# Unpaced gathers, an opening in two SBUF regions, and first layer-1 strips ahead, in a sparse two-layer graph kernel

## The chip, the cores and the metric

The kernel runs on one core of one Trainium2 chip. The metric is device time in microseconds of one execution. Before the change it was 2570.24 us, the median of 14 runs (2565.58 to 2576.75).

## The reference

A graph of 3327 nodes with 128 features goes through two layers, each with a layer norm and a ReLU ahead of it and a residual around it. Layer 0 is an attention layer (GATv2) of four heads over a weighted adjacency; layer 1 is a graph convolution over the same adjacency.

```python
h = maximum(layernorm(x), 0)
# layer 0, for each of 4 heads
E = leaky_relu((h @ w1)[:, None, :] + (h @ w2)[None, :, :], 0.01)
s = exp(tanh((E @ a) / 8) * 8) * adj
out = leaky_relu((s / s.sum(-1, keepdims=True)) @ h @ Wlin.T, 0.01)
x = x + concatenate(outs, -1) @ w
# layer 1
h = maximum(layernorm(x), 0)
A_t = adj + eye(n);  D_inv = rsqrt(A_t.sum(1))
x = x + relu((D_inv[:, None] * A_t * D_inv[None, :]) @ (h @ W.T + b))
```

About 2% of the adjacency is not zero, so a node has some 64 neighbours. Scores are needed for those pairs only.

## The kernel before, in words

Nodes are padded to 3328 = 26 blocks of 128. Layer 0 goes block by block, and each block is done in two halves (`hb`) of 64 rows. For a half, the neighbours' rows are gathered from a table in device memory by indirect DMA, which GpSimd (POOL) issues. A table row holds 720 floats (2880 B): 64 edge weights, 128 features of the node, a few scalars, and the four projections `h @ w2`. There are two such tables, one for each half: the features are the same, but the 64 edge weights in front are rewritten for each block (`weights`, L554: a DMA on SP's queue that reads the transposed adjacency `AT_d` and writes the first 256 B of every row).

The neighbour lists of a half fill 32 gathers of 128 rows, in 4 windows (`w`) of 8 gathers, and 3 more gathers (`ge`) hold what overflows: 35 a half, 70 a block, 1820 in all. A window's 8 gathers land in one buffer `g` of 23040 bytes a partition; there are 4 such buffers in the pool `pg`, and one of `ge`. A window is two groups (`m`) of TensorE work, the overflow one, so a half has 9 groups and a block 18. A group is:

- `stage_z` (L562): TensorE transposes the gathered projections into PSUM (`z`, L573), and VectorE takes the maximum with `x1n` (`r`, L585, 128x1024 at a time, two in a group).
- `stage_r` (L591): TensorE multiplies `r` with the score vector (`s`, L597).
- `finish` (L601), a generator in steps: copy, transpose, tanh and exp, weights `wt`, and the aggregation `ag` (L645, L663), after which the buffer is free (`allow`).
- `close` (L669), another generator, once a half or block is aggregated: output projection, residual, layer norm of layer 1, its product with `W`, and at last (L736) the block's rows of layer 1's right side into `x_sb`. The block is then `closed`.

Beside the groups of one block runs `prep` of the next (72 steps, half a block ahead): load of its adjacency rows (`load`, L334, 1.7 MB into the single buffer `adjb`), transposes of it to `AT_d`, the sparse index lists by repeated maxima of eight, and small products.

The order is written out by hand (`manual_schedule`): every engine runs its instructions in the order of the program. The function `slot` (L806) is called six times a group; it takes a step of every open `finish` and `close`, advances `prep`, and calls `fetch` and `trickle`. `fetch` (L770) puts the gathers of a window into `queue` when a buffer is free. `trickle` (L795) issues from the queue by a credit of `RATE = 0.7` gathers a slot, and `issue` (L788) makes each gather wait for the latest maximum `r` in program order (`state["pace"]`).

```python
def trickle():
    state["credit"] = min(2.0, state["credit"] + RATE) if queue else 0.0
    while queue and (state["credit"] >= 1 or queue[0][0] is None):
        state["credit"] -= queue[0][0] is not None
        issue()
```

In the opening (pool `pre`) the node features are normalised, and for 7 groups of four blocks `features`, `turn`, `products` (L971) and `store` (L967) make the table rows in `img` (5 buffers) and write each to both tables (1312 KB each), on SP's queue. `AT_d` of block 0 and the first two `weights` come before. When `pre` closes, `pg` is opened in its place.

Layer 1 (`layer1`, L859) multiplies strips: for each strip `s` of four blocks (512 columns of `AT_d`), one matmul (L870) for each column block `j` that is not in the partial sum `part1` already (`finished`: the blocks closed before the strip's rows were prepared). That is 26, 24, 20, 16, 12, 8 and 4, or 110 column blocks of 256 KB. They are loaded in pieces of up to 11 into `g` buffers (`strip`, L820) once the last gathers are issued, and multiplied while the last block is being closed and after it. The last column of strip 0 waits until every block is closed.

Of the kernel before, what the change touches and what calls it, by code (L numbers as in the profile page):

```python
# [227 lines left out]
def _sparse_layers(tc, nc, x, adj, w1, w2, a, wlin, w, gw, gb, gb_sb, gwT, x_sb, dinv, flag, ident, out):  # L228
# [24 lines left out]
    with ExitStack() as l0:  # L253
# [4 lines left out]
        xn_d = dram.tile([NP, D], F32, name="xn_d")  # L258
        part1_d = dram.tile([D, NP], F32, name="part1_d")
        NS = -(-NB // 4)  # L260
        AT_d = dram.tile([NS * NP, 4 * P], F32, name="AT_d")
# [76 lines left out]
        def prep(b, k):  # L338
# [6 lines left out]
            def tables_step(j0):  # L345
                n = min(4, NB - j0)
                pt = ps_tr.tile([P, 4, P], F32, name="tr")
                for q in range(n):
                    nc.tensor.transpose(pt[:, q, :], adjb[:, (j0 + q) * P:(j0 + q + 1) * P], ident)  # L349
                at = pat.tile([P, 4, P], F32, name="at") if b else blks[0].pool.tile([P, 4, P], F32, name="at0", bufs=4)  # L350
                nc.scalar.copy(at[:, :n, :], pt[:, :n, :])  # L351
                at0 = (b // 4) * NP
                eng = nc.scalar if b else nc.sync
                eng.dma_start(AT_d[at0 + j0 * P:at0 + (j0 + n) * P, b % 4 * P:b % 4 * P + P].rearrange("(b p) c -> p b c", p=P),
                                  at[:, :n, :])
                js = range(min(n, finished(b) - j0))
                if len(js):
                    known.append(known_step(j0, js, at))
# [56 lines left out]
            k.turned = True  # L415
            hTb = pb.tile([P, P], F32, name="hTb")
            nc.sync.dma_start(hTb, hT_d[:, b * P:(b + 1) * P])
            nc.scalar.activation(adjb, adjb, AF.Copy, accum_out=deg)
# [115 lines left out]
            nc.scalar.copy(pex, pm[:, :16 * H].rearrange("p (t h) -> p t h", h=H))  # L534
            k.x1b, k.x1n, k.pex, k.hTb = x1b, x1n, pex, hTb
            yield

        def gather(b, hb, w):

            k = blks[b]  # L540
            tab = tables[hb]
            if w == NW:
                g, n, at = pe_.tile([P, OVT, ROW], F32, name="ge"), OVT, k.idxo[:, hb]
            else:
                g, n, at = pg.tile([P, WT, ROW], F32, name="g"), WT, k.idx[:, w, WT * hb:WT * hb + WT]

            def one(t):
                return nc.gpsimd.indirect_dma_start(out=g[:, t, :], out_offset=None, in_=tab[:, :],  # L548
                                                    in_offset=bass.IndirectOffsetOnAxis(ap=at[:, t:t + 1], axis=0))

            queue.extend((k, hb, w, partial(one, t)) for t in range(n))
            k.g[hb, w] = g
# [9 lines left out]
        def stage_z(k, hb, m, slot):  # L562
# [4 lines left out]
            for hp in range(2):  # L567
# [15 lines left out]
                else:  # L583
                    r0 = HALF * hb + 32 * (m % 2)
                    made = nc.vector.tensor_tensor(r.rearrange("p h (i s) -> p h i s", s=16), z.rearrange("p h (i s) -> p h i s", s=16),  # L585
                                            k.x1n[:, 2 * hp:2 * hp + 2, r0:r0 + 32, None].to_broadcast([P, 2, 32, 16]), OP.max)
                    state["pace"] = made.ins.name
                out.append(r)
# [165 lines left out]
        state = {"slot": 0, "fetched": 0, "g": 4, "ge": 1}  # L754
        state["pace"], state["credit"] = None, 0.0
        RATE = 0.7
        SYNC = mybir.DependencyInfo(mybir.DependencyClass.Sync, mybir.DependencyReason.DATA)
        ends, tails = [], []
# [29 lines left out]
        def issue():  # L788

            what, _, _, make = queue.popleft()  # L790
            made = make()
            if what is not None and state["pace"] is not None:
                tc.add_manual_dep(made.ins, state["pace"], SYNC, reason="pace")

        def trickle():  # L795
            state["credit"] = min(2.0, state["credit"] + RATE) if queue else 0.0
            while queue and (state["credit"] >= 1 or queue[0][0] is None):
                state["credit"] -= queue[0][0] is not None
                issue()
# [6 lines left out]
        def slot():  # L806
# [5 lines left out]
            fetch()  # L812
            trickle()


        PIECE = 11
        pieces = [(s, j0, min(PIECE, NB - j0)) for s in range(NS) for j0 in range(finished(4 * s), NB, PIECE)]
        strips = {}

        def strip(s, j0, n):  # L820
            g = pg.tile([P, WT, ROW], F32, name="g")
            v = g.rearrange("p t c -> p (t c)")[:, :n * 4 * P].rearrange("p (j i) -> p j i", j=n)
            w = min(4, NB - 4 * s) * P
            for k, lo in enumerate(range(0, n, 4)):
                hi = min(n, lo + 4)
                eng = nc.scalar if k % 2 else nc.sync
                eng.dma_start(v[:, lo:hi, :w], AT_d[s * NP + (j0 + lo) * P:s * NP + (j0 + hi) * P, :w].rearrange("(j p) i -> p j i", p=P))
            strips[s, j0] = v

        def strip_in(s):  # L830
# [6 lines left out]
            if finished(4 * s):  # L837
                nc.sync.dma_start(r1[:, 0], part1_d[:, rows].rearrange("p (b i) -> p b i", b=n))
            return n, rows, r0, r1

        def strip_out(s, po, n, rows, r0, r1):

            ot, t, xo = r0[:, 1], r1[:, 1], r0[:, 0]
            po = po[:, :n * P].rearrange("p (b i) -> p b i", b=n)
            if finished(4 * s):
                nc.vector.tensor_add(ot, po, r1[:, 0])
            else:
                nc.scalar.copy(ot, po)
# [10 lines left out]
        def layer1():  # L859
            ending = []  # L860
            for s in range(NS):
                w = min(4, NB - 4 * s) * P
                po = ps_z.tile([P, 2, BANK], F32, name="z")[:, 0]
                j1 = finished(4 * s)
                ins = strip_in(s)
# [11 lines left out]
            for e in ending:  # L877
                for _ in e:
                    pass

        groups = [(b, hb, m) for b in range(NB) for hb in range(2) for m in range(NG)]
        fetches = [(b, hb, w) for b in range(NB) for hb in range(2) for w in range(NW + 1)] + [(NB, 0, i) for i in range(len(pieces))]

        with tc.tile_pool(name="pre", bufs=1) as pre:
            blks[0].pool = pre
            w2_sb = pre.tile([P, H, D], F32, name="w2_sb")
            nc.scalar.dma_start(w2_sb, w2.rearrange("h k d -> k h d"))
            a_bc = pre.tile([P, H, D], F32, name="a_bc")
            spans = [(lo, min(hi, NB)) for lo, hi in ((0, 4), (4, 12), (12, NB)) if lo < NB]
            x_v = x.rearrange("(b p) d -> p b d", p=P)  # L890
            for lo, hi in spans:
                nc.sync.dma_start(x_sb[:, lo:hi, :], x_v[:, lo:hi, :])
# [15 lines left out]
            wa = pre.tile([P, 3 * H], F32, name="wa")  # L908
            zero = pre.tile([1, ROW // 6], F32, name="zero")
            nc.vector.memset(zero, 0.0)  # L910
            nc.sync.dma_start(tables[0][NP:NP + 1, :].rearrange("r (k u) -> r k u", k=6), zero[:, None, :].to_broadcast([1, 6, ROW // 6]))
            nc.sync.dma_start(tables[1][NP:NP + 1, :].rearrange("r (k u) -> r k u", k=6), zero[:, None, :].to_broadcast([1, 6, ROW // 6]))

            def norm(b0, n):
# [10 lines left out]
                for _ in inv_root(rstd, var):  # L925
                    pass
                cen = pre.tile([P, n, D], F32, name=f"cen{b0}")
                for k in range(n):
# [6 lines left out]
            def weights_of_scores():  # L935


                prod = pre.tile([P, H, D], F32, name="prod")
                nc.vector.tensor_mul(prod, w2_sb, a_bc)
# [9 lines left out]
            def features(i):  # L949

                b0, n = 4 * i, min(4, NB - 4 * i)
                img = pre.tile([P, 4, ROW - FEAT], F32, name="img", bufs=5)
                nc.gpsimd.memset(img[:, :n, P + H:PROJ - FEAT], 1.0)
# [4 lines left out]
            def turn(i):  # L958
                b0, n = 4 * i, min(4, NB - 4 * i)
                pt = ps_s.tile([P, BANK], F32, name="s")  # L960
                for k in range(n):
                    nc.tensor.transpose(pt[:, k * P:(k + 1) * P], imgs[i][:, k, :P], ident)
                hTs[i] = pre.tile([P, BANK], F32, name="hT", bufs=2)
                nc.scalar.copy(hTs[i][:, :n * P], pt[:, :n * P])
# [6 lines left out]
            def products(i):  # L971
# [18 lines left out]
                store(i, 0)  # L990
                if i:
                    store(i - 1, 1)

            wlin_sb = pre.tile([P, H, D], F32, name="wlin_sb")
            nc.sync.dma_start(wlin_sb, wlin.rearrange("h o d -> o h d"))
# [23 lines left out]
            with tc.manual_schedule():  # L1019
# [18 lines left out]
                weights(0, 1)  # L1038
                turn(0)
                weights_of_scores()  # L1040
                if len(spans):
# [8 lines left out]
                for i in range(1, K):  # L1050
# [3 lines left out]
                    advance(2 + NCODE * i / (K - 1))  # L1054
                    ahead(i + 4)
                store(K - 1, 1)
                advance(NLIST)
                turn_parameters()
                if NB > 1:
                    load(1)  # L1060
                advance(NPREP)

        pg = l0.enter_context(tc.tile_pool(name="pg", bufs=4))

        with tc.manual_schedule():
# [5 lines left out]
            for i in range(-1, n + 1):  # L1071
                if i + 1 < n:
                    slot()
                if 0 <= i < n:
                    b, hb, m = groups[i]
                    rs[i] = stage_z(blks[b], hb, m, slot)
                if 0 <= i - 1 < n:
# [6 lines left out]
            todo = "one"  # L1084
            while ends or tails:
                slot()
# [143 lines left out]
```

## Time and profile before

| | |
|---|---|
| median of 14 runs | 2570.24 us (2565.58 to 2576.75) |
| the profiled execution | 2572.91 us; its span, first to last instruction, 2571.2 us |
| mean granted TensorE clock | 0.978 |
| busy share | PE 89%, DVE 79%, POOL 70%, ACT 27% |
| DMA | 867.74 MB, mean 337 GB/s |
| DMA queues, share of 16 engines | gathers (q0) 71.8%, SP (q1) 18.4%, ACT (q10) 7.1% |
| first gather starts, last gather ends | 85.6 us, 2435.5 us |

PE, PEld, DVE, ACT, POOL and SP are TensorE's matmuls, its weight loads, VectorE, ScalarE, GpSimd and the sync engine. A line of the costliest groups reads: line, engine, operation, out<-in, count | busy us, mean ns of one | idle time of the engine just before them, and what ended most of it. "issue" means that the engine waited for nothing that the profile shows. A line of the timeline has start and duration in us, and in brackets the idle time before it and its releaser. A line of the waits has total us, times, and the longest. A line of the stages has the stretch and its length, then busy us and number of instructions of each engine, the granted clock, the DMA share and GB/s. A line of the chain has start, length, and the work on it.

### The profile page before, as it was taken

How to read it: one execution, taken by the hardware profiler on the slowest of the kernel's cores; microseconds unless marked ns; L12 is line 12 of the kernel's file. 1: busy time of each engine (PE TensorE's matmuls, PEld its weight loads, DVE VectorE, ACT ScalarE, POOL GpSimd, SP SyncE). 2: the span in 40 equal slices, each digit the busy share in tenths (PEclk: the TensorE clock that was granted, in tenths of full speed). 3: DMA queues.
4: the chain of work that ended last, by engine and by line, in shares of the span. 5: the costliest groups of instructions: out<-in, count | busy, mean ns of one | idle time of the engine just before them, and what ended most of it. 6: DMA issues, size and time to landing. Idle time of an engine off the chain costs nothing.

```text
span 2571.2 us, 52428 instructions
## 1 busy us (share of the span) xinstructions
PE 2291.4 (89%) x19410; PEld 1594.4 (62%) x19410; DVE 2027.1 (79%) x6256; ACT 700.6 (27%) x1648; POOL 1796.0 (70%) x1865
## 2 busy tenths in 40 slices
PE   6689998888988998999999999899999989998898
PEld 3456666665666666666666666667666666766543
DVE  5788988788887878879888888878888788896512
ACT  3222233223223322322322232232223223222110
POOL 3577777777777777777777777777777777777600
PEclk8699999999999999999999999999999999999999
DMA  9999999999999999999999999999999999999976
GB/s 316 353 350 330 351 361 331 339 365 347 324 352 350 332 343 365 334 333 355 356 331 341 375 337 337 359 353 329 342 371 334 329 354 351 337 316 325 308 270 216
DMA packets 459768, 867.74 MB, mean 337 GB/s; under 512 B 208877, under 2 KB 317937, under 8 KB 456177
## 3 DMA queue, kind: packets, MB, share of 16 engines
q0 software_dynamic: 145600, 671.04, 71.8%
q1 hardware_dynamic: 217360, 136.76, 18.4%
q10 hardware_dynamic: 96544, 56.50, 7.1%
q8 instruction: 156, 2.56, 0.4%
q14 instruction: 108, 0.88, 0.1%
HBM read 795.84 MB, written 112.63 MB: 353 GB/s over the span
## 4 chain that ended last, share of the span: by engine, by line
DVE 28%; DMA 27%; PE 25%; POOL 10%; issue 9%; ACT 0%; DVEq 0%; SPq 0%; ACTq 0%; POOLq 0%
DMA g<-table,idx 20%; DVE r L585 12%; POOL g L548 8%; PE z L573 7%; DMA ge<-table,idxo 4%; PE s L597 4%; DVE cand L399 4%; PE z L870 4%; PE z L576 3%; DVE codes L395 2%; PE tr L614 2%; DMA AT_d<-at 1%; PE ag L645 1%; POOL ge L548 1%; PE tr L496 1%
## 5 line engine op out<-in xcount | busy, mean ns | idle before, releaser
L548 POOL DMA_INDIRECT g<-table,idx x1664 | 1618.5, 973 | 558.1 <-issue 359.3
L573 PE MATMUL z<-ident,g 128*128 128x128 f32 x6656 | 929.7, 279 | 184.5 <-DVE r L585 121.6
L585 DVE TENSOR_TENSOR r<-z,x1n 128x1024 f32<-128x1024 f32 x832 | 1009.3, 1215 | 32.7 <-PE z L573 30.5
L573 PEld LDWEIGHTS z<-ident,g 128*128 128x128 f32 x6656 | 746.2, 143 | 395.2 <-DVE r L585 248.3
L597 PE MATMUL s<-r,sel 128*32 128x512 f32 (+1 forms) x3744 | 489.2, 595 | 0.7 <-ACT ssb L605 0.7
L617 DVE TENSOR_TENSOR sc<-tr,g 128x32 f32<-128x32 f32 x208 | 38.6, 186 | 328.4 <-PE tr L614 328.4
L605 ACT COPY ssb<-s 128x512 f32<-128x512 f32 x260 | 146.9, 565 | 513.9 <-PE s L597 509.2
L399 DVE MAX8 cand<-codes 128x8 f32<-128x52 uint16 x1664 | 215.4, 205 | 0.0
L548 POOL DMA_INDIRECT ge<-table,idxo x156 | 154.9, 993 | 47.5 <-issue 35.9
L625 ACT ACTIVATE th<-sc 128x32 f32<-128x32 f32 x260 | 58.3, 224 | 446.8 <-DVE sc L620 441.1
L576 PE MATMUL z<-oi,x1b 128*128 128x384 f32 x416 | 175.0, 503 | 0.0
L645 PEld LDWEIGHTS ag<-g,wt 128*32 128x32 f32 x3328 | 98.8, 110 | 113.4 <-issue 98.9
L351 ACT COPY at<-tr 128x512 f32<-128x512 f32 (+1 forms) x182 | 101.0, 555 | 221.1 <-PE tr L349 187.6
L614 PE MATMUL tr<-ident,ssb 128*128 128x128 f32 x988 | 154.6, 277 | 4.4 <-ACT ssb L605 3.0
L573 PEld LDWEIGHTS z<-ident,ge 128*128 128x128 f32 x624 | 82.0, 147 | 108.2 <-DMA ge<-table,idxo 34.8
L582 ACT ACTIVATE r<-z 128x768 f32<-128x768 f32 x104 | 84.4, 811 | 217.7 <-PE z L576 217.7
L597 PEld LDWEIGHTS s<-r,sel 128*32 128x32 f32 x3744 | 73.8, 108 | 110.0 <-issue 85.9
L573 PE MATMUL z<-ident,ge 128*128 128x128 f32 x624 | 114.4, 284 | 30.3 <-DMA ge<-table,idxo 27.9
L645 PE MATMUL ag<-g,wt 128*32 128x133 f32 x3328 | 133.5, 278 | 0.0
L614 PEld LDWEIGHTS tr<-ident,ssb 128*128 128x128 f32 x988 | 115.6, 142 | 14.2 <-ACT ssb L605 12.5
L349 PE MATMUL tr<-ident,adjb 128*128 128x128 f32 x676 | 106.6, 280 | 16.4 <-DMA adjb<-in_adj_dram 10.2
L395 DVE SCALAR_TENSOR_TENSOR codes<-adjb,code 128x832 uint16<-128x832 f32 x104 | 102.3, 1021 | 1.5 <-DMA adjb<-in_adj_dram 1.5
(177 smaller groups left out, 2343.8 us busy)
## 6 DMA issues: line engine op xcount, KB each, us to landing
adjb<-in_adj_dram SPq DMA_DIRECT2D x26, 1664.0 KB
table<-AT_d SPq DMA_DIRECT2D x52, 832.0 KB
AT_d<-at ACTq DMA_DIRECT2D x150, 256.0 KB
g<-table,idx POOLq DMA_INDIRECT x1664
table<-img SPq DMA_DIRECT2D x12, 1312.0 KB
g<-AT_d SPq DMA_DIRECT2D x11, 1024.0 KB
g<-AT_d ACTq DMA_DIRECT2D x9, 1024.0 KB
g<-AT_d SPq DMA_DIRECT2D x7, 768.0 KB
```

The source lines that it names most:

```text
L349: nc.tensor.transpose(pt[:, q, :], adjb[:, (j0 + q) * P:(j0 + q + 1) * P], ident)
L395: nc.vector.scalar_tensor_tensor(codes[:, i], adjb[:, c0:c0 + part], 0.0, code[:, c0:c0 + part], op0=OP.not_equal, op1=OP.mult, accum_out= ...
L399: nc.vector.max(cand[:, c, 8:].rearrange("p (r s) -> p r s", s=32)[:, :, sgm % 32], codes.rearrange("p a b -> p (a b)")[:, sgm % 32 * SEG: ...
L548: return nc.gpsimd.indirect_dma_start(out=g[:, t, :], out_offset=None, in_=tab[:, :], in_offset=bass.IndirectOffsetOnAxis(ap=at[:, t:t + 1 ...
L573: nc.tensor.matmul(z[:, i, q * P:(q + 1) * P], g[:, m % 2 * 4 + q, PROJ + h * D:PROJ + (h + 1) * D], ident, is_transpose=True, start=(q == ...
L576: nc.tensor.matmul(z[:, i, :n], k.x1b[:, h * D:(h + 1) * D], k.oi[:, hb * n:(hb + 1) * n], start=False, stop=True, skip_group_check=True)
L585: made = nc.vector.tensor_tensor(r.rearrange("p h (i s) -> p h i s", s=16), z.rearrange("p h (i s) -> p h i s", s=16), k.x1n[:, 2 * hp:2 * ...
L597: nc.tensor.matmul(k.s[32 * h:32 * h + 32, :n], sel[:, h, 31 - at:63 - at], rs[h // 2][:, h % 2, :n], start=(at == 0), stop=(at == 1 or m ...
L605: nc.scalar.copy(ssb[:, :nk * P], s[:, :nk * P])
L614: nc.tensor.transpose(pt[:, q, :], ssb[:, q * P:(q + 1) * P], ident)
L645: nc.tensor.matmul(ag[32 * cg:32 * cg + 32, u, :WORK], wt[:, t].rearrange("p h q -> p (h q)"), g[:, t, FEAT:FEAT + WORK], start=(w == 0 an ...
L870: nc.tensor.matmul(po[:, :w], x_sb[:, j, :], strips[s, j - at][:, at, :w], start=(j == j1), stop=(j == NB - 1))
```

## The change

It has three parts.

1. `RATE`, the credit and the dependency on the latest maximum are taken out: `trickle` issues everything that `fetch` has put into the queue. The order of the gathers on POOL stays.
2. The opening's tiles are put in two pools, `pre` and `post` (`post`: four of the five `img` buffers and `prod`), and the four gather buffers become four pools of one buffer each (`pgs`, used in turn), so that the first two stand where `pre` was and the other two where `post` was. Table 1's stores of groups 2 to 6 are issued after all of table 0's and after `load(1)`, that of group 5 (whose `img` is in `pre`) first; `features` is called one group later (`ahead(i + 3)`); block 0's `hTb` is loaded early.
3. A generator `begin` is started at the first group of the second half of block 24 (of 0 to 25) and stepped once a slot. It multiplies columns 0 to 23 of strip 0 and 2 to 13 of strip 1, six columns at a time: one 1.5 MB load into the `adjb` buffer, 8 slots, then a matmul every three slots, with the sum in one `ps_tr` bank. The sums go to `part2_d` in device memory and are added in `strip_out`. `layer1` starts these two strips behind those columns, so 74 column blocks in 11 pieces are left to it.

```diff
         def issue():
-            what, _, _, make = queue.popleft()
-            made = make()
-            if what is not None and state["pace"] is not None:
-                tc.add_manual_dep(made.ins, state["pace"], SYNC, reason="pace")
+            queue.popleft()[-1]()
 
         def trickle():
-            state["credit"] = min(2.0, state["credit"] + RATE) if queue else 0.0
-            while queue and (state["credit"] >= 1 or queue[0][0] is None):
-                state["credit"] -= queue[0][0] is not None
+            while queue:
                 issue()
...
+        SHORT = 6
+        early = {}
+        for s, runs in ((0, 4), (1, 2)):
+            if NB > SHORT * runs + 1 + finished(4 * s):
+                early[s] = (finished(4 * s), finished(4 * s) + SHORT * runs)
+
+        def begin():
+            for s in early:
+                po = bank()
+                for j0 in range(*early[s], SHORT):
+                    v = pa.tile([P, NP], F32, name="adjb")[:, :SHORT * BANK].rearrange("p (j i) -> p j i", j=SHORT)
+                    nc.sync.dma_start(v, AT_d[s * NP + j0 * P:s * NP + (j0 + SHORT) * P, :].rearrange("(j p) i -> p j i", p=P))
+                    for _ in range(8):
+                        yield
+                    for j in range(j0, j0 + SHORT):
+                        assert blks[j].closed
+                        nc.tensor.matmul(po, x_sb[:, j, :], v[:, j - j0, :], start=(j == early[s][0]), stop=(j == early[s][1] - 1))
+                        yield
+                        yield
+                        yield
+                part2 = pv.tile([P, H, P], F32, name="outT").rearrange("p h i -> p (h i)")
+                nc.scalar.copy(part2, po)
+                nc.sync.dma_start(part2_d[:, 4 * s * P:4 * s * P + BANK], part2)
+                yield
...
+            blks[0].at = [pre.tile([P, 4, P], F32, name=f"at{i}") for i in range(4)]
+            cens = {lo: pre.tile([P, hi - lo, D], F32, name=f"cen{lo}") for lo, hi in spans}
+            turned = [pre.tile([P, BANK], F32, name=f"hT{i}") for i in range(2)]
+            prod = post.tile([P, H, D], F32, name="prod")
+            room = [(post if i else pre).tile([P, 4, ROW - FEAT], F32, name=f"img{i}") for i in range(5)]
...
-                if i:
-                    store(i - 1, 1)
+                if i < 2:
+                    store(i, 1)
...
-                    ahead(i + 4)
-                store(K - 1, 1)
+                    ahead(i + 3)
+                if NB > 1:
+                    load(1)
+                for i in sorted(range(2, K), key=lambda i: i % 5 > 0):
+                    store(i, 1)
                 advance(NLIST)
                 turn_parameters()
-                if NB > 1:
-                    load(1)
                 advance(NPREP)
...
-        pg = l0.enter_context(tc.tile_pool(name="pg", bufs=4))
+        pgs = [l0.enter_context(tc.tile_pool(name=f"pg{i}", bufs=1)) for i in range(4)]
...
+                    if (b, hb, m) == (NB - 2, 1, 0):
+                        state["early"] = begin()
```

## The prediction

> **What bounds the kernel now.** I read the page first, then the waits of POOL, its timeline, busy time by stage, the waits of PE near the end, and the chain of the last 130 us.
>
> ```profile
> PE 2291.4 (89%) x19410; PEld 1594.4 (62%) x19410; DVE 2027.1 (79%) x6256; ACT 700.6 (27%) x1648; POOL 1796.0 (70%) x1865
> L548 POOL DMA_INDIRECT g<-table,idx x1664 | 1618.5, 973 | 558.1 <-issue 359.3
> ```
>
> By share of busy time PE leads and POOL, at 70%, looks free. The second line corrects that: 558.1 us of POOL's idle time lies just before its 1664 gathers, mostly released by nobody ("issue"). The timeline of POOL shows what that is:
>
> ```profile
> 85.57 1.24 POOL L548 DMA_INDIRECT g<-table,idx  x1 [29.06 <-DVE rel L502]
> 87.11 0.95 POOL L548 DMA_INDIRECT g<-table,idx  x1 [0.30 <-issue]
> 88.36 0.95 POOL L548 DMA_INDIRECT g<-table,idx  x1 [0.30 <-issue]
> ...
> 2433.35 0.95 POOL L548 DMA_INDIRECT ge<-table,idxo  x1 [0.30 <-issue]
> 2434.60 0.94 POOL L548 DMA_INDIRECT ge<-table,idxo  x1 [0.30 <-issue]
> ```
>
> A gather takes 0.95 us and the next starts 0.30 us later: one per 1.25 us. The first 35, issued before any maximum exists, are not paced and have the same 0.30. So the gap belongs to the instruction, not to the pace. 1820 gathers x 1.25 = 2275 us; the stream runs from 85.6 to 2435.5 = 2350 us. Adding up every gather, the other 75 us are 53 of longer gathers (up to 1.76 us each) and 22 of gaps beyond 0.30. POOL issues without a break for 91% of the span: it is the bound, and the time is opening (85.6) + stream (2350) + tail (135.7), with 1.7 us between span (2571.2) and profiled time (2572.9). That run lies 2.7 above the median, 2570.2.
>
> **Pacing removed.** What the pace can cost is within the 22 us of extra gaps, in 30 places (longest 3.1 us). The waits of POOL:
>
> ```profile
> POOL g L548 <- DMA g<-table,idx: 42.0, 137, 0.5
> POOL g L548 <- DVE r L585: 27.2, 74, 3.1
> POOL ge L548 <- DMA g<-table,idx: 3.3, 11, 0.3
> ```
>
> Most of these are the fixed 0.30 with a late event beside it (74 x 0.30 = 22 of the 27 us). Gather by gather, some 6 us lie where a maximum came last, 7 where PE had not yet freed the buffer, 9 where the eighth gather before had not landed (a gather waits for its semaphore's previous one; landing takes 6.3 us on average, up to 11). Only the first kind goes; part of the second, if PE starts earlier. The order of POOL's instructions stays. The weights' DMAs leave FIFO earlier on SP and wait there for the same landings. Value -5; ends -22 (all extra gaps) and +10 (unspaced issue doubles the landing waits).
>
> **Opening.** Now `pg` opens over all of `pre`: the first gather waits for every table store of both halves. By the landing records table 0 is complete at 79.2, table 1 at 84.3; the index list is there at 73.4. After the change five of the seven table-1 stores are behind all of table 0, and two gather buffers need only the first region. Table 0's 7 stores with 2 of table 1 are 8.5 full stores at some 3.8 us each (landing to landing), from 36.4: complete near 69. The indices follow the products, about 5 us earlier: near 68. First gather near 70, or 77 if the second buffer's image store (i = 5) gates both: 9 to 15 us earlier.
>
> But the third window needs the second region, so all stores. SP now has `load(1)` ahead of five stores, and `load(1)` waits for ACT's read of the old block (L418, now 64.7 to 67.6): the stores are queued behind that, while DMA still works off table 0. DMA is the limit here:
>
> ```profile
> 35.00:85.00 50.00, 31.89 (x124) 20.83 (x123) 28.12 (x135) 16.54 (x31) 7.33 (x13) 0.74 1.04 395
> 85.00:100.00 15.00, 9.58 (x35) 7.08 (x34) 7.78 (x29) 1.98 (x5) 11.39 (x11) 0.50 0.83 270
> ```
>
> (The last three columns are granted clock, DMA share and GB/s.) 395 GB/s until the stores are in, then 270 with gathers alone. The first 16 gathers (16 x 128 x 2880 B = 5.9 MB) move ahead of the last stores: at 395 GB/s 14.9 us. Stores and adjacency load, which land at 88.5 now, then land near 103.4, and gather 17 starts there, against 85.6 + 16 x 1.25 = 105.6 now. So 10 to 15 us of earlier start shrink to about -2; with idle PE and DVE time of blocks 0 to 3 used sooner (block 1's adjacency lands some 14 us earlier, and 7.7 us of the extra gaps are in blocks 1 to 3) -4. Ends: -15 (stores not delayed by gathers) and +3 (AT_d's writes of block 1, 1.7 MB or 4.3 us, come in as well). I take the low end because the trace has the two queues together: while the next adjacency load runs (120 to 125), the gathers' packets move 0.88 MB in 5 us, against 1.56 in the 5 us before.
>
> A rule that speaks against this part: the Trainium skill, "DMA: Bandwidth & Descriptors", section "Queues, rings and completion order", says that each DMA engine takes turns between queues by packets. By that rule early gathers simply delay the stores (-2); by a first-come order, which no run here shows, the part would be worth -15. The zero rows in 3 pieces instead of 6, the earlier `hTb`, and the tiles that move pools cost nothing that waits: none is on POOL, and SP's queue holds only stores then.
>
> **First strips ahead.** 36 columns (24 of strip 0, 12 of strip 1) leave the tail:
>
> ```profile
> 2454.93 7.73 PE z L870 x18
> 2463.25 2.77 PE z L870 x6
> 2467.38 6.01 PE z L870 x14
> 2473.61 1.72 PE z L870 x4
> 2476.22 2.58 PE z L870 x6
> ...
> 2484.39 6.04 PE z L870 x8
> 2490.86 20.60 PE z L870 x48
> ```
>
> This is the chain at the end. A column is two records, so 20.60/24 = 0.858 us. Until 2484.4 (closing of the last block, L736) PE does 25 columns, between the steps of the closing and in front of them; then 85. After the change 74 are left: one before the closing ends, 73 after: 12 x 0.858 = -10.3. The closing loses its 24 other matmuls, 20.6 us, from its way; its own steps (L645, L663, L685, L696, L707 with their copies) fill about half of that: -12, ends 0 and -18. The strips' 19 MB (74 x 256 KB) load in 50 us at 395 GB/s, under 63 us of matmuls. Tail: -22 (-10 to -28).
>
> What it costs ahead: 36 x 0.858 = 30.9 us of PE, 9.4 MB of DMA, two copies and two 256 KB stores and loads, over the last 27 groups (2305 to 2436), where no next block is prepared:
>
> ```profile
> 2305.00:2436.00 131.00, 114.54 (x995) 77.74 (x998) 80.76 (x157) 27.14 (x71) 99.16 (x104) 0.97 0.93 307
> ```
>
> and PE's waits in the same window:
>
> ```profile
> PE z L573 <- DMA g<-table,idx: 15.3, 14, 3.1
> ```
>
> PE idles 131 - 114.5 = 16.5 us, 15.3 of it waiting for gathers, that is for POOL. DMA has 307 of 395 GB/s; 72 more fit. If PE's busy time held no slack, the groups would end 30.9 - 16.5 = 14.4 us later; the transposes step by 0.11 us where nothing is waited for, though 420 of them are busy 61.6 us, so there is slack, and 0 is the other end. On top: each of the six loads is a 1.5 MB DMA started 8 slots (8 x 0.81 = 6.5 us) ahead of its matmul; the 1.7 MB adjacency load at 119.2 landed after 10.2 us. PE, in order, would stand for up to 3.7 us six times with the z transposes queued behind, and one `ps_tr` bank of two is held for a whole strip. Stands that fall into waits for gathers are free. Value +8 (0 to +35).
>
> **Sum.** -5 - 4 - 22 + 8 = -23: 2572.9 - 23 = 2549.9 as profiled, 2547 against the median.
>
> **Rivals.**
> 1. Slower: PE becomes the bound of the last 1.5 blocks. Price: 14.4 + 6 x 3.7 = 36.6 us, and a few more at the held bank: with the tail's -22 and nothing from opening and pace, +15: 2585. It decides once the groups end over 31 us later. For it: PE 87% busy there; against: in that window PE waits only 0.8 us for DVE before z (its weight loads 8.5). Chance 0.13.
> 2. Only the tail pays (DMA takes back the opening, POOL stays back to back): -22 + 8 = -14: 2556. For it: POOL's fixed 0.30. Chance 0.2.
> 3. The opening keeps its start and the strips hide fully: -15 - 5 - 22 = -42: 2528. Against: 395 GB/s. Chance 0.18.
> 4. The change removes a pace that never binds, and strips ahead cost what they save: 2570. Chance 0.07, the same-case (0.2%, 5 us, is what a measurement of this kernel tells from no change).
>
> **Numbers.** Forecast 2547, chance 0.42. Faster 0.80, same 0.07, slower 0.13. Range 2522 to 2573: from a little beyond rival 3 to just over no change; it leaves out most of rival 1 and the best ends together.
>
> **What would show it.** Right: gathers still 1.25 us apart; first gather near 70 to 77 but the 17th at 100 to 106; last gather 5 to 15 us earlier than 2435.5, unless PE delays it in the last block; about 115 us from the last gather to the end; waits of PE for early strips of a few us. Wrong: gathers closer than 1.25 us; gaps over 2 us inside the stream before block 24 (a new bound); the last 27 groups over 150 us long; a tail over 125 us.

## The result and the profile after

The changed kernel is slower: 2598.45 us, median of 10 runs (2589.46 to 2603.4), beside 2571.61 us for the kernel before; the ratio is 1.0100, 95% interval 1.0087 to 1.0113. The profiled execution took 2588.82 us (its span is 2587.0), just below the fastest of these ten. The forecast was 2547 (2522 to 2573), so sign and range are wrong; what happened is the mechanism of rival 1. For the runs below: the kernel before took about 2570 us on the chips of this result, of e1 to e4, e17 and e18, and 3150 to 3200 us on the five chips of e5 to e16, so each run is compared only with the kernel before on its own chip.

The page of the changed kernel, its busy line and two groups, and then the second of these groups in the page before:

```profile
PE 2291.4 (89%) x19410; PEld 1595.4 (62%) x19410; DVE 2028.5 (78%) x6258; ACT 700.2 (27%) x1649; POOL 1792.2 (69%) x1865
L555 POOL DMA_INDIRECT g<-table,idx x1664 | 1615.1, 971 | 594.8 <-issue 453.9
L592 DVE TENSOR_TENSOR r<-z,x1n 128x1024 f32<-128x1024 f32 x832 | 1010.1, 1215 | 91.1 <-PE z L580 89.1
L585 DVE TENSOR_TENSOR r<-z,x1n 128x1024 f32<-128x1024 f32 x832 | 1009.3, 1215 | 32.7 <-PE z L573 30.5
```

No engine is busy for more than 1.4 us longer than before (PE 2291.4 us in both), so the time is standing, not work. The maxima (L592, L585 before) wait 91.1 us, nearly all of it for PE's transposes; before it was 32.7. The timeline of POOL:

```profile
78.74 1.18 POOL L555 DMA_INDIRECT g<-table,idx  x1 [24.84 <-DMA table<-img]
80.22 0.95 POOL L555 DMA_INDIRECT g<-table,idx  x1 [0.30 <-issue]
...
98.32 0.94 POOL L555 DMA_INDIRECT g<-table,idx  x1 [0.30 <-ACT at L352]
99.56 0.94 POOL L555 DMA_INDIRECT g<-table,idx  x1 [0.30 <-issue]
...
2464.38 0.95 POOL L555 DMA_INDIRECT ge<-table,idxo  x1 [0.30 <-issue]
```

The stream begins 6.8 us earlier (78.74 for 85.57), the 17th gather is at 99.56 with nothing ahead of it but the fixed 0.30, and gathers still start 1.24 to 1.25 us apart. Yet the last one ends at 2465.3, 29.8 us later than 2435.5. Busy time by stage (engines PE, PEld, DVE, ACT, POOL, then granted clock, DMA share, GB/s) shows where:

```profile
35.00:85.00 50.00, 33.22 (x128) 21.71 (x127) 31.74 (x145) 17.42 (x34) 13.10 (x19) 0.75 1.03 391
85.00:100.00 15.00, 9.88 (x59) 7.55 (x59) 7.43 (x32) 1.76 (x3) 11.35 (x13) 0.68 1.03 406
2305.00:2436.00 131.00, 97.54 (x686) 59.41 (x686) 51.83 (x98) 17.40 (x45) 71.13 (x76) 0.87 0.81 274
```

From 85 to 100 the DMA engines now carry gathers and stores together (406 GB/s; 270 before). From 2305 to 2436 everything is emptier than before: PE 97.5 us (114.5), POOL 71.1 (99.2), DMA 274 GB/s (307). An emptier chip at the place where work was added means that something stands. PE's waits from 2284 to 2472 name it:

```profile
PE tr L847 <- DMA adjb<-AT_d: 40.6, 5, 11.8
PE z L580 <- DMA g<-table,idx: 0.8, 1, 0.8
```

L847 is the early matmul of layer 1. PE used to wait here for gathers (15.3 us); now it waits for the early loads, and 6.8 us more at the sixth, behind this stretch. Such a wait, in which PE stands idle, is called a stand below. PE's timeline has the six, each with its stand in brackets:

```profile
2316.51 2.07 PE L847 MATMUL tr<-adjb,x_sb 128*128 128x512 f32 x2 [11.79 <-DMA adjb<-AT_d]
2348.31 2.07 PE L847 MATMUL tr<-adjb,x_sb 128*128 128x512 f32 x2 [8.19 <-DMA adjb<-AT_d]
2378.49 2.08 PE L847 MATMUL tr<-adjb,x_sb 128*128 128x512 f32 x2 [5.49 <-DMA adjb<-AT_d]
2408.54 2.07 PE L847 MATMUL tr<-adjb,x_sb 128*128 128x512 f32 x2 [5.45 <-DMA adjb<-AT_d]
2442.92 2.08 PE L847 MATMUL tr<-adjb,x_sb 128*128 128x512 f32 x2 [9.73 <-DMA adjb<-AT_d]
2473.09 2.08 PE L847 MATMUL tr<-adjb,x_sb 128*128 128x512 f32 x2 [6.84 <-DMA adjb<-AT_d]
```

Together 47.5 us. The waits of SP's queue (2270 to 2500) show what the early loads (L842) wait for, and those of POOL (2235 to 2470) that it waits for PE:

```profile
SPq L842 <- PE tr L847: 67.1, 4, 17.0
SPq L842 <- DMA adjb<-AT_d: 52.5, 4, 20.9
```

```profile
POOL g L555 <- issue: 45.9, 113, 11.8
POOL g L555 <- PE ag L651: 39.5, 8, 9.9
```

There is one `adjb` buffer. SP can issue a load only when PE's last matmul on the load before is done; it lands 13 to 15 us later (the first, issued 0.6 us behind a `weights` DMA on the same queue, after 27), and PE comes to it some 7 us after the issue (15 for the first). Behind the standing PE no buffer `g` comes free, so POOL waits for the aggregation (`ag`, L651) in its turn, which it never did in this stretch before. The chain at the end shows the same, then the tail:

```profile
2428.46 14.41 DMA adjb<-AT_d
2442.92 2.08 PE tr L847 x2
...
2459.82 13.23 DMA adjb<-AT_d
2473.09 2.08 PE tr L847 x2
...
2494.84 0.85 PE s L603 x8
...
2511.68 2.09 PE z L903 x2
2516.15 10.22 DMA r<-part_d
2528.59 17.17 PE z L903 x40
```

The last group's scores end at 2495.7, 91.3 us ahead of the end; before, they ended at 2452.7, 118.5 ahead:

```profile
2451.85 0.85 PE s L597 x8
```

The account between the two profiles: the first gather of block 24 starts 18.1 us earlier (2240.9 for 2259.0); from there to the groups' end it is 254.8 us for 193.7, +61.1; from there to the end -27.2. Together +15.8, the difference of the spans.

### The profile page after: what moved, and what is told of

Its sections match the earlier page's. It is cut to its first block, busy times and chain, and to the rows that moved or that the text cites. A ratio compares the mean times of both kernels' runs of the same rounds, so it can differ in the third digit from the quotient of the medians.

```text
span 2587.0 us, 51877 instructions
## 1 busy us (share of the span) xinstructions
PE 2291.4 (89%) x19410; PEld 1595.4 (62%) x19410; DVE 2028.5 (78%) x6258; ACT 700.2 (27%) x1649; POOL 1792.2 (69%) x1865
## 4 chain that ended last, share of the span: by engine, by line
PE 29%; DVE 25%; DMA 24%; POOL 13%; issue 8%; ACT 1%; DVEq 0%; SPq 0%; ACTq 0%; POOLq 0%
DMA g<-table,idx 12%; DVE r L592 11%; POOL g L555 11%; PE z L580 8%; PE s L603 5%; DMA ge<-table,idxo 4%; DMA adjb<-AT_d 4%; PE z L583 3%; DVE cand L400 3%; DMA AT_d<-at 2%; PE z L903 2%; PE tr L620 2%; PE tr L847 2%; DVE codes L396 2%; PE ag L651 2%
## 5 line engine op out<-in xcount | busy, mean ns | idle before, releaser
L592 DVE TENSOR_TENSOR r<-z,x1n 128x1024 f32<-128x1024 f32 x832 | 1010.1, 1215 | 91.1 <-PE z L580 89.1
L555 POOL DMA_INDIRECT ge<-table,idxo x156 | 154.1, 988 | 47.5 <-issue 34.7
L651 PEld LDWEIGHTS ag<-g,wt 128*32 128x32 f32 x3328 | 98.8, 110 | 114.4 <-issue 100.3
L603 PEld LDWEIGHTS s<-r,sel 128*32 128x32 f32 x3744 | 73.9, 108 | 112.4 <-issue 86.8
L651 PE MATMUL ag<-g,wt 128*32 128x133 f32 x3328 | 133.5, 278 | 0.8 <-DVE wt L642 0.8
L350 PE MATMUL tr<-ident,adjb 128*128 128x128 f32 x676 | 106.9, 281 | 20.5 <-DMA adjb<-in_adj_dram 10.3
```

The lines of the kernel that those rows point to most:

```text
L603: nc.tensor.matmul(k.s[32 * h:32 * h + 32, :n], sel[:, h, 31 - at:63 - at], rs[h // 2][:, h % 2, :n], start=(at == 0), stop=(at == 1 or m ...
L651: nc.tensor.matmul(ag[32 * cg:32 * cg + 32, u, :WORK], wt[:, t].rearrange("p h q -> p (h q)"), g[:, t, FEAT:FEAT + WORK], start=(w == 0 an ...
```

## Experiments

Three theories of the loss. Theory A: the six loads into one buffer make PE stand. Theory B: the 31 us of early matmuls, in a PE with little idle time, and the PSUM bank that they hold. Theory C: unspaced gathers and the new opening cost something later. Times are medians, beside the kernel before on the same chip. In the diffs, "..." marks what is left out.

### The parts one by one (e1 to e4)

One chip, the kernel before at 2570.03 us (23 runs).

e1, the change without strips ahead:

```diff
-        for s, runs in ((0, 4), (1, 2)):
+        for s, runs in ():
```

> The changed kernel without the strips ahead (parts 1 and 2 stay). Theory A (the six early loads make TensorE stand, and that is all that costs): the lead of 18 us that the changed kernel's gathers have at block 24 reaches the end, so 18 us less than the kernel before, 2553. Theory B (the early matmuls themselves are too much work for TensorE): the same 2553. Theory C (unspaced gathers or the new opening cost something that shows only later): not below 2565. First gather near 79, last gather near 2418.

Measured: 2558.86 us (6 runs), ratio 0.9956 (0.9940 to 0.9972).

e2, the new opening alone (e1 with the pace put back):

```diff
+                    state["pace"] = made.ins.name
...
+                tc.add_manual_dep(made.ins, state["pace"], SYNC, reason="pace")
```

> The opening in two regions alone: paced gathers, no strips ahead. From the profiles of before and after: the first gather starts 6.8 us earlier and block 2 6.6 us earlier, so 2564 if nothing is given back (-7). If the paced stream takes the lead back through its landing waits: 2571. If the opening is also what makes blocks 3 to 23 shorter: 2555.

Measured: 2565.04 us (12 runs), 0.9981 (0.9969 to 0.9992).

e3, the kernel before with only the pace taken out:

```diff
...
         def trickle():
-            state["credit"] = min(2.0, state["credit"] + RATE) if queue else 0.0
-            while queue and (state["credit"] >= 1 or queue[0][0] is None):
-                state["credit"] -= queue[0][0] is not None
+            while queue:
                 issue()
```

> The pace alone taken out of the kernel before; old opening, no strips ahead. From the profiles: blocks 3 to 23 gained 11 us of gaps on POOL, so 2560 (-11) if that is the pace's doing; 2566 (-5) by the prediction's term; 2571 if the pace never binds; above 2575 if gathers that are not spaced make the landing waits longer.

Measured: 2563.75 us (12 runs), 0.9978 (0.9965 to 0.9991).

e4, the kernel before with only the strips begun ahead (`begin` and what belongs to it, as in the change):

```diff
...
+                    if (b, hb, m) == (NB - 2, 1, 0):
+                        state["early"] = begin()
```

> The strips ahead alone, on the kernel before with its pace and its opening. Theories A and B: the whole loss is here, groups end 60 us later and the tail is 27 us shorter, so 2571 + 33 = 2604, up to 2616 by the medians. Theory C: below 2590. By the prediction's sum (-22 + 8): 2557.

Measured: 2603.78 us (5 runs), 1.0143 (1.0122 to 1.0165).

What follows: pace -6.3, opening -5.0, both -11.2: the two add up, and theory C falls on this chip. The strips ahead cost 34 us alone, and the waits of PE in e4 (2284 to 2500; its early matmul is L853) have stands of nearly the same sum as in the full change (46.2 us in six, 47.5 there), so the other two parts have no hand in them:

```profile
PE tr L853 <- DMA adjb<-AT_d: 46.2, 6, 10.4
PE z L577 <- DVE r L589: 0.6, 1, 0.6
```

### Loads or matmuls, on chips that answer another question (e5 to e16)

Three kernels to tell A from B. *One load*: matmuls, banks and short tail as in the change, five loads gone; the later runs of six multiply the first load's columns again, so strips 0 and 1 are not computed.

```diff
                 for j0 in range(*early[s], SHORT):
-                    v = pa.tile(...)
-                    nc.sync.dma_start(v, ...)
+                    if s == 0 and j0 == 0:
+                        v = pa.tile(...)
+                        nc.sync.dma_start(v, ...)
```

*Lead 14*: the same loads, with more time ahead of the matmuls and less between them.

```diff
-                    for _ in range(8):
+                    for _ in range(14):
                         yield
...
                         nc.tensor.matmul(po, x_sb[:, j, :], v[:, j - j0, :], ...)
                         yield
                         yield
-                        yield
```

*Ring*: the six columns of the buffer are used as a ring; each is loaded again (256 KB) right after its own matmul. The first matmul comes after 16 slots, and then one every four.

```diff
+            for i in range(SHORT):
+                take(i)
+            for _ in range(16):
+                yield
+            for i, (s, j) in enumerate(todo):
...
+                nc.tensor.matmul(po, x_sb[:, j, :], v[:, i % SHORT, :], ...)
+                if i + SHORT < len(todo):
+                    take(i + SHORT)
+                for _ in range(4):
+                    yield
```

First chip, before at 3153.81 us:

> The changed kernel with all early matmuls in their places but one early load instead of six: the later five runs multiply the first run's columns again (strips 0 and 1 of the result are wrong). Theory A (standing for loads): five of the six stands go, about 40 us, and with TensorE's work left 2598 - 40 = 2558. Theory B (30.9 us of matmuls and the held PSUM bank): not below 2590.

> The changed kernel with 14 slots instead of 8 between an early load and its first matmul, and a matmul every two slots instead of three, so that a run of six stays 26 slots long. Theory A: each stand is shorter by 6 slots of 0.6 to 0.8 us, six times 3.6 to 4.8 us, so 2573 to 2577. Theory B: 2598, the same work in the same number of slots.

> The changed kernel with the early columns in a ring of six single columns in the same buffer: each column is loaded again (256 KB) as soon as its matmul has been issued, 24 slots before it is needed; a matmul every four slots, the same 36 columns and the same bytes. Theory A: the stands go but for the first, so the groups end some 45 us earlier than in the changed kernel: 2553, and faster than the kernel before by some 18 us. Theory B: 2590 or more.

Measured: one load 3232.83 (1.0258, 1.0222 to 1.0293), lead 14 3242.24 (1.0295, 1.0256 to 1.0334), ring 3237.69 (1.0258, 1.0228 to 1.0287).

Second chip, before at 3150.21 us, with e1's kernel beside them:

> The same kernel as e5_one_load (one early load, 36 early matmuls, wrong columns in five of six runs), again, since e5 to e7 ran on a chip on which the kernel before takes 3154 us and POOL waits for TensorE throughout. On a chip like that of e1 to e4, theory A (standing for loads): 2558; theory B (the matmuls' own time and the held bank): not below 2590.

> The same kernel as e7_ring, on a chip like that of e1 to e4. Theory A: TensorE's stands shrink to a few us in all, the groups end 14 us later than without the strips ahead, the tail is 27 us shorter: 2559 - 13 = 2546. Theory B: 2590 or more.

> The same kernel as e6_lead14, on a chip like that of e1 to e4. Theory A: 2573 to 2577 (six stands, each shorter by 6 slots of 0.6 to 0.8 us). Theory B: 2598.

> The same kernel as e1_no_ahead, beside the other three as their reference without strips ahead. On a chip like that of e1 to e4 2559. On a chip where the kernel before takes 3154 us: if the loss there is the strips' too, within 1% of the kernel before; if pacing or opening cost something where TensorE is the bound, 2% above it.

Measured: one load 3259.35 (1.0316, 1.0280 to 1.0351), ring 3248.49 (1.0305, 1.0273 to 1.0337), lead 14 3249.33 (1.0290, 1.0259 to 1.0321), no strips ahead 3266.82 (1.0363, 1.0334 to 1.0393).

Third chip, before at 3197.17 us:

> The change with one early load in place of six: the later runs of six columns multiply the first run's columns again, so that matmuls, held banks and short tail stay and only the reloading goes (the output of layer 1 is then not the reference's). Theory A (the six loads into the one buffer make the PE stand, 47.5 us in the profile of after): most of the 34 us that the strips cost alone goes, and the kernel takes about 2558 us where before takes about 2570; what stays is one load's stand and the 31 us of matmuls against the 27 us of tail. Theory B (the 31 us of early matmuls in a PE that has little idle time left, and the PSUM bank that they hold, are the cost): the time stays at 2590 us or above. The comparison counts where before takes about 2570 us; where it takes about 3150 us the gathers do not bound the kernel and neither theory is tested.

> The change with the six columns of the early buffer used as a ring: each column of 256 KB is loaded again as soon as its own matmul is done, and a matmul comes every 4 slots, so that six loads stand ahead of the matmuls. All the work is done. Theory A: no stand of the PE at the loads, 2546 us (2559 of the kernel without strips ahead, 14 us of matmuls beyond the PE's idle time, 27 us of tail off), which would be the fastest of all. Theory B: 2590 us or above.

> The change with 14 slots instead of 8 between an early load and its first matmul, and a matmul every 2 slots instead of 3. All the work is done. Theory A: a slot takes 1.25 to 1.5 us, so the 14 slots cover 17 to 21 us where the loads landed after 13 to 27 us; stands of 47.5 us shrink to 20 or 25, the time to 2573 to 2577 us. Theory B: no difference from the change, 2598 us.

Measured: one load 3325.17 (1.0398, 1.0369 to 1.0427), ring 3322.59 (1.0383, 1.0346 to 1.0420), lead 14 3328.07 (1.0407, 1.0385 to 1.0430).

Fourth and fifth chip, before at 3199.05 and 3188.91 us, the ring alone:

> The ring of single columns once more, wanted beside a run of before of about 2570 us: every column of 256 KB is loaded again right after its own matmul, a matmul every 4 slots, six loads ahead. Theory A (the PE stands for the six loads into one buffer): the stands for that buffer fall from 47.5 us to a few, and the kernel takes about 2546 us. Theory B (the matmuls themselves and the bank they hold): 2590 us or above. Where before takes about 3150 us nothing is told.

> The ring of single columns again, for a comparison with a before of about 2570 us: each column of 256 KB is loaded again right after its own matmul, a matmul every 4 slots, six loads ahead. Theory A (the PE stands for the six loads into one buffer): stands for that buffer of a few us instead of 47.5, and about 2546 us. Theory B (the matmuls themselves and the bank they hold): 2590 us or above. Where before takes about 3150 us nothing is told.

Measured: 3326.36 (1.0393, 1.0347 to 1.0439) and 3320.63 (1.0419, 1.0371 to 1.0466).

What follows for A and B: nothing. The page of e15 says why:

```profile
L555 POOL DMA_INDIRECT g<-table,idx x1664 | 1626.5, 977 | 1210.5 <-PE ag L651 676.9
```

There the gathers idle 1210.5 us, more than half of it waiting for PE to free a buffer, in every block; a block takes some 120 us instead of 90, and the granted clock is 0.915 instead of 0.978. Where POOL waits for PE all the time, it is not the bound, and the comparison that was wanted is not made. But these runs do show that the gain of the first two parts is not general: e11, which has only those, is 3.6% slower than before on its chip. Beside e11, the three kernels with strips ahead are 7 to 18 us faster on that chip. Which of the two parts costs there, and by what, was not taken apart and stays open; the prediction's picture of POOL as the bound does not hold on these chips.

### The ring where POOL is the bound (e17)

> The ring of single columns again: each column of 256 KB is loaded again right after its own matmul, a matmul every 4 slots, six loads ahead. Beside a before of about 2570 us: theory A (the PE stands for the six loads into one buffer) expects stands of a few us and 2546 us; theory B (the matmuls themselves and the bank they hold) 2590 us or above. Beside a before of 3150 to 3200 us: about 3.9% above it, as in the earlier runs, and nothing told of A and B.

Measured, on the chip of e1 to e4: 2537.74 us (4 runs), before 2572.29; ratio 0.9875 (0.9847 to 0.9902). It is the fastest kernel of the study, 21 us under e1. Its waits of PE (2230 to 2440; the early matmul is L853), and its busy time by stage:

```profile
PE z L580 <- DMA g<-table,idx: 2.1, 6, 0.6
PE z L580 <- DVE r L592: 1.8, 3, 0.6
PE tr L853 <- DMA adjb<-AT_d: 0.9, 1, 0.9
```

```profile
2305.00:2436.00 131.00, 129.26 (x1013) 81.48 (x1012) 74.84 (x138) 24.71 (x66) 91.24 (x96) 1.00 0.98 370
```

The same 36 columns, the same 9.4 MB, a bank held nearly as long (24 x 4 slots for strip 0, against 4 x 26): the stands fall from 47.5 us to 0.9, PE is busy for 129.3 of 131 us, DMA rises to 370 GB/s. The last lines of the scores in the chains of the ring and of e1 are these:

```profile
2445.04 0.85 PE s L603 x8
...
2437.86 0.85 PE s L603 x8
```

The groups end at 2445.9 for 2438.7 in e1, and 4.4 of these 7.2 us are there at block 24 already: the 30.9 us of matmuls cost 2.8. They fit because PE idled there: from block 24's first gather to the groups' end its idle time falls from 24.8 us in e1 to 6.3, and its busy time grows by 21.4, not 30.9 (both lines stand under e18); how the other 9.5 us come in was not taken apart. The tail is 91.6 us for 118.0, -26.4. So -26.4 + 2.8 = -23.6 from block 24 on, and 4.4 that came before: -19.2 between the spans (2537.5, 2556.7). On this chip e4, with the six loads, took 2603.78 us; less the 11.2 us of the first two parts, an estimate for the whole change here is 2593. Theory A holds; theory B, which asked for 2590 or above, falls. The kernel with one load, which keeps the matmuls' places exactly, was not run on such a chip.

### A longer lead with the same loads (e18)

> The change with 14 slots instead of 8 between an early load and its first matmul, and a matmul every 2 slots instead of 3; the one buffer and the six loads stay, all the work is done. Beside a before of about 2570 us. Theory A, with the 2538 us that the ring gave as the time without stands: a slot is 88 us / 108 = 0.81 us while the gathers set the pace, 14 of them 11.4 us; the loads landed after 13 to 15 us and the first after 27, so stands of 16 + 5 x 2.5 = 28 us are left of 47.5, of which the 16 us of PE's idle time may take some: 2550 to 2566 us. Theory B, already hardly tenable after the ring (the matmuls and the bank are the cost): 2590 us or above, as in the change. Beside a before of 3150 to 3200 us nothing is told.

Measured: 2563.07 us (12 runs), before 2568.97; 0.9977 (0.9963 to 0.9992). PE's waits from 2270 to 2460, and three of the four stands in its timeline:

```profile
PE tr L847 <- DMA adjb<-AT_d: 19.9, 4, 9.0
```

```profile
2371.18 2.07 PE L847 MATMUL tr<-adjb,x_sb 128*128 128x512 f32 x2 [4.18 <-DMA adjb<-AT_d]
2422.57 1.12 PE L847 MATMUL tr<-adjb,x_sb 128*128 128x512 f32 x2 [2.24 <-DMA adjb<-AT_d]
2447.86 1.56 PE L847 MATMUL tr<-adjb,x_sb 128*128 128x512 f32 x2 [4.47 <-DMA adjb<-AT_d]
```

The stands are shorter than the 28 us expected, since two of the five later loads landed after 7.2 and 8.2 us. Stands of 0.9, 19.9 and 47.5 us give 288.7, 315.1 and 346.1 us from block 24's first gather to the end (ring, lead 14, change): each microsecond of stand costs 1.2 to 1.4. The spacing of the matmuls does not follow this order (4, 2 and 3 slots), so it is not what sets the time. The longer lead takes back 35 of the 61 us between the medians of the change and the ring, and four of six loads still come late: with one buffer, a load cannot be issued before its forerunner's last matmul, however long the lead.

Each stand costs more than itself: 57.4 - 46.6 = 10.8 us in the change, 26.4 - 19.0 = 7.4 here. Busy time by stage, from block 24's first gather to the groups' end, in the change, lead 14, the ring and e1, shows where:

```profile
2240.90:2495.70 254.80, 202.03 (x1528) 128.15 (x1528) 125.51 (x271) 41.32 (x110) 133.55 (x140) 0.90 0.80 272
2244.60:2467.30 222.70, 195.99 (x1518) 124.52 (x1520) 124.10 (x267) 40.73 (x106) 133.49 (x140) 0.95 0.90 311
2248.80:2445.90 197.10, 190.83 (x1518) 122.43 (x1520) 123.83 (x267) 40.31 (x105) 134.03 (x140) 0.99 0.96 349
2244.40:2438.70 194.30, 169.47 (x1446) 115.25 (x1448) 123.23 (x267) 39.83 (x104) 134.00 (x140) 0.95 0.94 316
```

For the same work PE is busy 11.2 us longer in the change than in the ring, and 5.2 us longer in lead 14, at a mean granted clock of 0.90, 0.95 and 0.99. That is all of the 10.8 and most of the 7.4.

## Why the prediction was wrong, step by step

- **What bounds the kernel**: right for the chips where before takes about 2570 us. The gap of 0.30 us is the instruction's own; without the pace gathers came no closer than 1.24 us.
- **Pacing -5** (ends -22, +10): e3 measured -6.3. In its profile the extra gaps up to block 24 fell from 22.5 to 11 us (15.3 in e1's profile); the doubled waits for landings did not come (POOL's waits for the landing of gathers `g`: 42.0 us before, 10.5 in e3).
- **Opening -4** (ends -15, +3): e2 measured -5.0. The first gather came at 78.7, where 77 had been worked out for the case that the store of the sixth group (i = 5) gates it: that store landed at 77.6. The 17th gather came at 99.6, not 103.4: the last store landed at 98.0 (84.3 before), just ahead of it. So the delay was real: the last store came nearly 14 us later. But stores and adjacency load together were in at 98.0, 9.5 us later than the 88.5 before, where the bytes said 14.9. The rule of the Trainium skill, "DMA: Bandwidth & Descriptors", section "Queues, rings and completion order", that the queues are served in turn by packets, agrees: between 85 and 100 us both moved at once, at 406 GB/s. By first come, first served the part would have been worth -15; it was not.
- **Tail -22** (ends -28, -10): the mechanism was right, the size near its far end: -27.2 in the change and -26.4 in the ring. The closing of the block takes 16.0 us without its matmuls (2495.7 to 2511.7) for 31.7 before, -15.7 where -12 had been put; what follows it takes 75.3 us for 86.8, -11.5 where -10.3 had been put. The new load of `part2_d` stands on the chain (10.2 us, at 2516), but PE stood only 0.4 us for it.
- **Early cost +8** (ends 0, +35): this step failed. It has two terms. The matmuls' own cost, between 0 and 14.4, is 2.8 in the ring: the low end, as the slack of the transposes suggested. The stands were sized at 3.7 us each and expected to fall mostly into waits for gathers; they were 7.9 us each on average, and they were paid in full.
  - *The size.* The eight slots were sized well: 6.5 us, and landing less stand is 6.7 on average for loads two to six. The landing was not: it was taken from a 1.7 MB adjacency load (10.2 us) and was 13.1 to 14.9, mean 13.9, for these five, and 27.1 for the first. That adjacency load was no exception: from block 2 on, all 24 of them landed in 9.2 to 10.9 us in the profile of before, beside the same stream of gathers. What differs is the shape. Such a load moves in 128 packets of 13312 B, an early load in 768 packets of 2048 B (its rows are 512 floats). No run here changed the packets alone, so that this is the reason is not shown.
  - *The overlap.* A stand is not free because PE idles elsewhere: those 15 us of idle were waits for gathers, and they disappear as soon as PE has more to do or is late. In the ring the matmuls alone leave 2.1 us of them, and beside the ring the change pays 57.4 us for 46.6 us of stands. POOL stands with PE: its gaps beyond 0.30 behind block 24's first gather are 48.6 us, where they were 0 before.
- **Sum**: with -11 for the first two parts (medians), -27 for the tail, and +61 for the groups, +23; measured between medians +27.
- **Rival 1** named the mechanism and its point: groups ending over 31 us later. They ended 43 us later on the clock (2495.7 for 2452.7) and 61 later counted from block 24, and the stretch from 2287 (2305 less the lead of 18) to the last gather is 178 us long, where over 150 had been named as the sign of a wrong step. It had the parts in the wrong proportion, 14.4 of matmuls and 22 of stands, where the runs have 2.8, and 57.4 for the stands with the slow matmuls behind them. An account of the two profiles alone (30.9 of matmuls + 47.5 of stands - 16.5 of idle = 61.9, measured 61.1) closes with a large share for the matmuls, and only the ring shows that this share is wrong.
- Its chance of 0.13 was too low: the trace had the single buffer, the 10.2 us landing against the 6.5 us of slots, and an in-order PE at 87%. A stand that is certain by one's own numbers belongs in the sum, not in the range.

## What to carry to other kernels

Work moved in front of a bound is cheap in busy time and dear in waits: 31 us of matmuls cost 3 us, six loads into one buffer that were started too late cost the whole gain and more. Before moving it, write down for each load when its buffer comes free, how long it takes to land (read from loads of the same shape and place: here 1.7 MB in 13 KB packets landed in 10 us and 1.5 MB in 2 KB packets in 14), and how long the engine takes to get there; if the last is shorter than the second, an in-order engine stands, and everything behind it. Reload each part of a buffer as its own reader finishes, instead of the whole after the last.

## What the hardware showed that was not expected

- The same kernel, before the change, took about 2570 us on some chips and 3150 to 3200 us on five others, at granted clocks of 0.974 to 0.982 in its runs beside e1 to e4, e17 and e18, and 0.904 to 0.915 in those beside e5 to e16. A clock lower by 7% does not explain a time longer by 23 to 24%; what does stays open.
- After a stand PE works slowly for a while. The pair of early matmul records takes 1.02 to 1.13 us where no stand lies just before it, 1.12 after one of 2.24 us, 1.56 and 2.07 after 4.5 and 4.2, and 2.07 or 2.08 after every stand from 5.45 us on; but in e4 it takes 2.08 after 2.94 us already, so the length of the stand alone does not decide. The granted clock from 2305 to 2436 was 0.87 with the stands, 0.97 before the change and 1.00 in the ring, where PE hardly stood (0.9 us).
- The landing of a load varies. The later 1.5 MB loads took 13.1 to 14.9 us in the change, 10.5 to 15.8 in e4 and 7.2 to 14.1 in lead 14. In the ring a column of 256 KB took 5.2 to 7.3 us for the last twelve, which were issued one by one, and 6.8 to 20 before, where up to six stood in the queue together.
